# Inverse square roots of the layernorms and of layer 3 in a four-layer kernel: twelve VectorE steps in place of ScalarE's Sqrt and VectorE's reciprocal

## The chip, the cores and the metric

The kernel runs on one core of one Trainium2 chip. A core has five engines, each with its own queue: PE (TensorE, matmuls), DVE (VectorE), ACT (ScalarE), POOL (GpSimd) and SP (SyncE, which here only issues DMAs). The metric is the device time of one execution in microseconds. Times are medians of several runs.

## The reference, cut to what matters

Four layers follow each other. Each adds an attention part and a feed-forward part to `x`, which has 4 batches of 256 tokens with 256 features. Both parts read a layernorm of `x`.

```python
def _layernorm(x, axis=-1, eps=1e-05):
    m = jnp.mean(x, axis=axis, keepdims=True)
    v = jnp.var(x, axis=axis, keepdims=True)
    return (x - m) / jnp.sqrt(v + eps)

x = x + _L0_xattn_ref(_layernorm(x), ctx_2048, mask)     # plain attention over the context
x = x + _L0_ffn_ref(_layernorm(x), ...)                  # 32 experts, top 8
x = x + _L1_xattn_ref(_layernorm(x), ctx_2048, ...)      # adds a mean over the context, then a layernorm with gamma and beta
x = x + _L1_ffn_ref(_layernorm(x), ...)                  # 8 experts, top 2, and a shared one
x = x + _L2_xattn_ref(_layernorm(x), ctx_2048, ...)      # 16 heads of 128, keys and queries normed
x = x + _L2_ffn_ref(_layernorm(x), ...)                  # 4 experts, top 1
x = x + _L3_xattn_ref(_layernorm(x), ctx_2048, ...)
x = x + _L3_ffn_ref(_layernorm(x), ...)                  # quantized weights and activations
```

The attention of layer 3 has 32 heads of 8 features, and 1601 keys for each batch. Each head of each query and key is divided by its root mean square:

```python
def _rmsnorm(t):
    return t * jax.lax.rsqrt(jnp.mean(t * t, axis=-1, keepdims=True) + EPS)   # EPS = 1e-6
k_raw = context @ Wk.T; v_raw = context @ Wv.T; q = x @ Wq.T
q = _rmsnorm(q); k = _rmsnorm(k)
attn = softmax(q k^T / sqrt(8)); out = attn v
```

So an inverse square root is needed for every token of every layernorm (two columns for a tile of 128 partitions by 2 tokens), for each head of each key of layer 3 (13 key tiles by 32 heads, 416 columns a batch) and for each head of each query (64 columns a batch).

## The kernel before, in words

The tile framework orders each engine's instructions when the kernel is built, by priorities and modelled costs. On the chip an engine runs its own list in that order and waits where an input is not there yet. An instruction that waits holds all that stand behind it on its engine.

`rstd` (lines 79 to 82) makes every inverse square root of the kernel before: a Sqrt on ScalarE with scale and bias, then VectorE's reciprocal. ScalarE must load a table of functions (`ACT_TABLE_LOAD` in the profile) when it goes from Exp or another function to Sqrt, and again on the way back.

`layernorm` (line 84) is called 24 times. For each half of a tile VectorE runs `bn_stats` and `bn_aggr`; `rstd` follows on two columns, and then two `tensor_scalar` write the normed halves (line 95). Its callers are `normed` (line 115; layers 0 and 1, whose xn tiles PE transposes into `tp_ln`), `l1_xattn` (line 1195; two layernorms a batch called y and z), `turned` in layer 2 (line 1338) and layer 2's FFN (line 969).

While layers 0 and 1 run, `l2_early` (line 1206) makes the keys and values of layer 2 as filling work for PE: product, copies on ScalarE, squares (`sq_early`, one buffer), a reduce (`ss_early`) and `rstd` on 13 columns. These calls of `rstd`, those of layer 2's own keys (line 1437) and of layer 0 (line 317) are the same in both kernels.

Layer 3 works on one batch after the other (`l3`, line 1729). For each batch it goes over 8 pairs (h, u), and for each over 7 pairs of key tiles: `scores` (matmuls into `s`, then Exp on ScalarE into `e`), `values` (matmuls of the step before into `o`), and then one step of a generator, `beside` (line 1972), which prepares the next batch and finishes the batch before. Its steps are:

- `l3_kv` (line 1668), one key tile a step: four matmuls (two for each accumulation) into a PSUM bank `b`, one copy to `kr` and two to `va`. After tiles 4, 9 and 12 `l3_squares` squares a group of 5, 5 or 3 tiles (on POOL in the loop, on ScalarE in the early part) and VectorE reduces it into `ss`. After all tiles POOL multiplies `kr` by the inverse roots in four pieces, and PE transposes `kr` into `kT`.
- `queries` (line 1779): normed x, four transposes, copy to `xT`, product with wq, copy to `qr`, squares on ScalarE, reduce, inverse roots, multiply, transposes, copy to `qT`.
- `norms` (line 1772): statistics and inverse roots of x for the layernorms. It is called for batch 0 ahead of the layer, for batches 1 to 3 at the start of loop b=0, and for single batches later.
- `ffn` (line 1865) for the batch before.

In the loop all PSUM banks of these steps come from one pool with one buffer (`bank`, line 1752):

```python
ps = es.enter_context(tc.tile_pool(name="a3p", bufs=1, space=PSUM))
def bank():
    return ps.tile([P, 512], F32, name="b3", tag="tp")
```

For b > 0 the Sqrt in `queries` (line 1810) takes the keys, the queries and two columns for the old batch's layernorm at once, 482 columns; the reciprocals come in pieces of 66, 208 and 208 (lines 1811 and 1816). The keys of batch 0 have a Sqrt and a reciprocal of 416 columns of their own (line 1697).

Of the kernel before, what the change touches and what calls it, by code (L numbers as in the profile page):

```python
# [11 lines left out]
F32 = mybir.dt.float32  # L12
# [4 lines left out]
I32 = mybir.dt.int32  # L17
AF = mybir.ActivationFunctionType
ALU = mybir.AluOpType
# [4 lines left out]
P = 128  # L24
# [34 lines left out]
class Kernel:  # L59
# [19 lines left out]
    def rstd(self, out, in_, scale, eps):  # L79

        self.nc.scalar.activation(out, in_, AF.Sqrt, bias=eps, scale=scale)
        self.nc.vector.reciprocal(out, out)

    def layernorm(self, out, x):

        nc = self.nc
        st = self.small.tile([P, 2, 6], F32, name="ln_st")
        mv = self.small.tile([P, 2, 2], F32, name="ln_mv")
        rs = self.small.tile([P, 2], F32, name="ln_rs")
        for q in range(2):  # L90
            nc.vector.bn_stats(st[:, q, :], x[:, q, :])
            nc.vector.bn_aggr(mv[:, q, :], st[:, q, :])
        self.rstd(rs, mv[:, :, 1], 1.0, self.eps5)
        for q in range(2):
            nc.vector.tensor_scalar(
                out[:, q, :], x[:, q, :], mv[:, q, 0:1], rs[:, q : q + 1],
                ALU.subtract, ALU.mult,
            )
# [1569 lines left out]
    def l3_kv(self, b, st, early):  # L1668


        nc = self.nc
        ctxT = self.ctx3
        pool = self.late3 if b % 2 else self.a3
        kr = st["kr"] = self.a3.tile([P, NM, D], F32, name="kr3")
        va = st["va"] = self.va3[b % 2]
        ss = st["ss"] = self.a3.tile([P, (NM + 2) * NH3 + 2], F32, name="ss3")
        for m in range(NM):
            copy = nc.scalar.copy if early() else nc.vector.tensor_copy
            tf = self.take()
# [3 lines left out]
            copy(kr[:, m, :].rearrange("p (h d) -> p h d", d=HD3), tp[:, :, :, 0])  # L1683
            for h in range(2):
                copy(
                    va[h][:, m, : 16 * (HD3 + 1)].rearrange("p (h e) -> p h e", e=HD3 + 1)[:, :, :HD3],
                    tp[:, h * 16 : (h + 1) * 16, :, 1],
                )
            if m in (4, 9, NM - 1):
                m0 = {4: 0, 9: 5}.get(m, 10)  # L1690
                self.l3_squares(st, kr[:, m0 : m + 1, :], m0, early())
            if m == NM - 1 and b < B - 1:
                self.ctx3 = self.load_ctxT(self.a3, b + 1, 1)
            yield
        if b == 0:
            nk = NM * NH3
            self.rstd(ss[:, :nk], ss[:, :nk], 1.0 / HD3, self.eps6)
        for m0, m1 in ((0, 4), (4, 8), (8, 12), (12, NM)):
            v = kr[:, m0:m1, :].rearrange("p m (h d) -> p (m h) d", d=HD3)
            f = ss[:, m0 * NH3 : m1 * NH3, None].to_broadcast([P, (m1 - m0) * NH3, HD3])  # L1700
            nc.gpsimd.tensor_tensor(v, v, f, ALU.mult)
        yield
        yield
        yield
        kT = st["kT"] = [pool.tile([P, MP], F32, name="kT3", bufs=2) for _ in range(2)]
        for m0 in range(0, NM, 4):
            for h in range(2):
                n = min(4, NM - m0)
                copy = nc.scalar.copy if early() else nc.vector.tensor_copy
                tp = self.take().rearrange("p (m k) -> p m k", k=P)  # L1710
                for m in range(n):
                    nc.tensor.transpose(tp[:, m, :], kr[:, m0 + m, h * P : (h + 1) * P], self.ident)
                copy(kT[h][:, m0 * P : (m0 + n) * P], tp[:, :n, :].rearrange("p m k -> p (m k)"))
                yield

    def l3_squares(self, st, v, m0, early, pool=None):

        n = v.shape[1]
        sq = (pool or self.a3).tile([P, 2 if pool else 5, D], F32, name="sqq3" if pool else "sq3")
        if early:  # L1720
            self.nc.scalar.activation(sq[:, :n, :], v, AF.Square)
        else:
            self.nc.gpsimd.tensor_tensor(sq[:, :n, :], v, v, ALU.mult)
        self.nc.vector.tensor_reduce(
            st["ss"][:, m0 * NH3 : (m0 + n) * NH3], sq[:, :n, :].rearrange("p m (h d) -> p (m h) d", d=HD3),
            AX.X, ALU.add,
        )

    def l3(self, first):

# [10 lines left out]
        with ExitStack() as es:  # L1741
# [30 lines left out]
            def norms(bs):  # L1772

                for b in bs:
                    stats(b)
                v = slice(bs[0], bs[-1] + 1)
                self.rstd(rs[:, v, :], mv[:, v, :, 1], 1.0, self.eps5)

            def queries(b, st, old=None, fill=lambda n: None):

                ss = st["ss"]
                nk, nq = NM * NH3, (NM + 2) * NH3
                if old is not None:
                    stats(old)
                    nc.vector.tensor_scalar(
                        ss[:, nq:], mv[:, old, :, 1], float(HD3), HD3 * (1e-5 - 1e-6), ALU.mult, ALU.add
                    )
                elif b:  # L1790
                    nc.vector.memset(ss[:, nq:], 1.0)
                xn = normed(b, rs[:, b, :])
                fill(0)
                tp = bank().rearrange("p (k q t) -> p k q t", k=2, q=2)
# [10 lines left out]
                        self.mm(tq[:, q, :], xT[:, k, q * P : (q + 1) * P], self.wq3[:, k, :], k == 0, k == 1)  # L1805
                qr = one.tile([P, 2, D], F32, name="qr3")
                nc.vector.tensor_copy(qr, tq)
                self.l3_squares(st, qr, NM, True, one)
                part = ss if b else ss[:, nk:nq]
                nc.scalar.activation(part, part, AF.Sqrt, bias=self.eps6, scale=1.0 / HD3)  # L1810
# [161 lines left out]
            def beside(b, st):  # L1972

                if b + 1 < B:
# [40 lines left out]
            for _ in queries(0, first, None, lambda n: [next(kv) for _ in range(FIRST3[n])]):  # L2015
                pass
            busy = True
            self.take = bank
# [208 lines left out]
```

## Time and profile before

| | |
|---|---|
| median of 3 runs | 2565.55 us (2564.33 to 2566.97) |
| the profiled execution | 2571.23 us, its span 2569.2 us |
| granted PE clock over the span | 0.973 |
| busy: PE, DVE, ACT, POOL | 2429.6, 1404.4, 1310.9, 837.8 us |
| table loads on ACT | 79 of 1283 ns each, 34 of them at line 81 |
| Sqrt of a layernorm (128x2), reciprocal of it | 297 ns and 161 ns |
| Sqrt of a query (128x482) | 697 ns |
| reciprocals of 66, 208 and 416 columns | 567, 1418 and 2747 ns |

The page of the profile gives shares and counts for one execution. The timeline gives each instruction's start and duration in microseconds from the span's start, and in square brackets the idle time of its engine before it with what ended that. A group row gives the shape, the count, the busy time in us and the mean of one in ns, and then the idle time before such instructions. The layers lie at about 0 to 370 us (layer 0), 370 to 625 (its last addition and layer 1), 640 to 1925 (layer 2) and 1925 to 2569 (layer 3).

### The profile page before, as it was taken

To read this page: it belongs to the slowest core of one execution; us is meant where nothing else is said; L and a number is where in the kernel's file an instruction comes from. 1 tells how busy PE (TensorE), PEld (TensorE's weight loads), DVE (VectorE), ACT (ScalarE), POOL (GpSimd) and SP (SyncE) were. 2 spreads that over 40 slices of the span, in tenths; PEclk is the share of its full clock that TensorE was granted. 3 is DMA by queue.
4 is the path that set the end of the run, shared out by engine and by line. 5 is a ranking of instruction groups with operands and counts; after the bars stand their busy time and mean duration, and the time that the engine had idled before them with its cause. 6 is when DMAs were issued, how large, how long until landed. Compare 5 with 4: busy or idle time off the path is not lost.

```text
span 2569.2 us, 47086 instructions
## 1 busy us (share of the span) xinstructions
PE 2429.6 (95%) x17607; PEld 1507.7 (59%) x17623; DVE 1404.4 (55%) x2915; ACT 1310.9 (51%) x3000; POOL 837.8 (33%) x1516
## 2 busy tenths in 40 slices
PE   8989987899989999999999999998999999999997
PEld 5777865777645555555555555565554544544553
DVE  5453534843567777777777777763324324334323
ACT  3234434533654545454545454423336766757875
POOL 1015644213345555555555555541011001011000
PEclk9999998989999999999999999998999999999998
DMA  7165574624601111111111111004310100000000
GB/s 252 49 211 163 169 151 146 216 91 138 225 18 48 48 48 48 47 47 48 47 48 48 47 48 48 9 1 176 125 56 28 35 1 28 6 1 2 6 6 5
DMA packets 96474, 188.45 MB, mean 73 GB/s; under 512 B 15401, under 2 KB 64297, under 8 KB 95050
## 3 DMA queue, kind: packets, MB, share of 16 engines
q1 hardware_dynamic: 80102, 146.50, 16.7%
q0 software_dynamic: 10416, 28.46, 4.6%
q10 hardware_dynamic: 5732, 10.49, 1.3%
q8 instruction: 143, 2.34, 0.4%
q14 instruction: 81, 0.66, 0.1%
HBM read 137.29 MB, written 48.11 MB: 72 GB/s over the span
## 4 chain that ended last, share of the span: by engine, by line
PE 84%; DVE 5%; ACT 3%; DMA 3%; issue 2%; POOL 1%; another core or an unknown queue 1%; SPq 0%; ACTq 0%; PEld 0%; POOLq 0%; DVEq 0%; PEldq 0%
PE s L77 25%; PE o L77 24%; PE fill L1241 3%; PE f2gu L77 3%; PE b L77 3%; PE f1gu L77 2%; PE acc L77 2%; PE tpq L77 2%; PE f0gu L77 2%; PE filly L1241 2%; PE tpkv L77 2%; PE av L77 2%; PE f0y L77 2%; PE f2y L77 1%; PE f1y L77 1%
## 5 line engine op out<-in xcount | busy, mean ns | idle before, releaser
L1487 ACT ACTIVATE p<-s,nmsm 128x448 f32<-128x448 f32 (+1 forms) x512 | 326.1, 643 | 381.4 <-PE s L77 247.5
L1943 ACT ACTIVATE e<-s 128x1024 f32<-128x1024 f32 (+1 forms) x448 | 404.2, 960 | 159.6 <-PE s L77 154.5
L77 PE MATMUL o<-pT,va 128*128 128x256 f32 (+2 forms) x1920 | 434.2, 379 | 9.4 <-DVE pT L1528 7.9
L77 PE MATMUL s<-kT,qT 128*32 128x448 f32 (+1 forms) x4096 | 427.3, 558 | 11.6 <-ACT kT L1459 8.2
L77 PEld LDWEIGHTS o<-pT,va 128*128 128x128 f32 (+1 forms) x1920 | 347.5, 192 | 130.4 <-issue 89.6
L1522 POOL TENSOR_SCALAR p<-p,rm 128x448 f32<-128x448 f32 (+1 forms) x512 | 323.1, 651 | 6.2
L1483 DVE TENSOR_REDUCE nmsm<-s 128x2 f32<-128x896 f32 (+1 forms) x256 | 287.5, 1123 | 7.9
L77 PE MATMUL s<-qb,kT 32*128 32x256 f32 (+1 forms) x3328 | 268.2, 405 | 13.2 <-ACT e L1943 11.0
L1528 DVE STREAM_TRANSPOSE pT<-p 128x896 f32<-128x896 f32 (+1 forms) x256 | 270.7, 1111 | 9.4 <-POOL p L1522 8.7
L77 PEld LDWEIGHTS s<-kT,qT 128*32 128x32 f32 x4096 | 120.2, 110 | 264.0 <-issue 239.0
L77 PE MATMUL o<-e,va 128*32 128x256 f32 (+1 forms) x3328 | 236.3, 392 | 1.2 <-DVE os L2040 1.2
L77 PEld LDWEIGHTS s<-qb,kT 32*128 32x128 f32 (+1 forms) x3328 | 163.4, 181 | 105.2 <-issue 75.5
L1515 POOL TENSOR_TENSOR rm<-em,tot 32x8 f32<-32x8 f32 x256 | 54.2, 212 | 400.8 <-DVE tot L1512 389.6
L1241 PE MATMUL fill<-wkc_early,ctxT 128*128 128x256 f32 (+1 forms) x572 | 146.2, 407 | 13.4 <-ACT kT_early L1277 12.6
L77 PEld LDWEIGHTS o<-e,va 128*32 128x32 f32 (+1 forms) x3328 | 90.6, 110 | 115.1 <-issue 75.0
L1970 POOL TENSOR_TENSOR x<-x,t 128x32 f32<-128x32 f32 x64 | 14.7, 251 | 439.7 <-DVE t L1965 439.7
L1480 DVE TENSOR_TENSOR s<-s,mask 128x128 f32<-128x128 f32 (+1 forms) x256 | 84.3, 330 | 104.7 <-PE s L77 92.5
L1241 PEld LDWEIGHTS fill<-wkc_early,ctxT 128*128 128x128 f32 (+1 forms) x572 | 114.4, 203 | 35.4 <-ACT kT_early L1277 14.8
L458 POOL DMA_INDIRECT f0xr<-f0xd,f0src x95 | 90.5, 953 | 70.6 <-PE f0tph L515 18.7
L1487 ACT ACTIVATION_READ_ACCUMULATOR p<-s,nmsm 128x1 f32 x512 | 101.4, 198 | 0.0
L77 PE MATMUL f2gu<-f2wgu,f2xsT 128*128 x176 | 85.5, 611 | 0.6 <-ACT f2xsT L74 0.3
L566 POOL DMA_INDIRECT f0yt<-f0yd,f0slot x64 | 62.3, 974 | 64.1 <-DVE x L558 33.4
(488 smaller groups left out, 3500.4 us busy)
## 6 DMA issues: line engine op xcount, KB each, us to landing
ctxT<-in_ctxT SPq DMA_DIRECT2D x9, 1664.0 KB
vd<-va_early SPq DMA_DIRECT2D x96, 128.0 KB
kd<-kT_early SPq DMA_DIRECT2D x48, 256.0 KB
kT<-kd SPq DMA_DIRECT2D x16, 768.0 KB
va<-vd SPq DMA_DIRECT2D x16, 768.0 KB
f0yd<-f0ys SPq DMA_DIRECT2D x95, 128.0 KB
wq<-in_l_wq SPq DMA_DIRECT2D x16, 512.0 KB
wo<-in_l_wo SPq DMA_DIRECT2D x16, 512.0 KB
```

Source lines behind the costliest of these rows:

```text
L77: self.nc.tensor.matmul(out, lhsT, rhs, start=start, stop=stop, **kw)
L458: nc.gpsimd.indirect_dma_start(out=t, out_offset=None, in_=xd[:, :], in_offset=bass.IndirectOffsetOnAxis(ap=src[:, n : n + 1], axis=0),)
L566: nc.gpsimd.indirect_dma_start(out=yt, out_offset=None, in_=yd[:, :], in_offset=bass.IndirectOffsetOnAxis(ap=slot[:, t, r : r + 1], axis=0),)
L1241: ins = nc.tensor.matmul(tp[:rows, t, :], ctxT[u // NKV2][:, k, c0 : c0 + rows], w[u % NKV2][:, k, :], start=k == 0, stop=k == 1,)
L1480: nc.vector.tensor_tensor(sv, sv, mask[:, 2 * c : 2 * c + 2, : nt - CT, :].rearrange("p n t i -> p n (t i)"), ALU.add)
L1483: nc.vector.tensor_reduce(ms[:, 0, 2 * c : 2 * c + 2], s[:, :, : nt * 32], AX.X, ALU.max, negate=True)
L1487: nc.scalar.activation(p[:, n, : nt * 32], s[:, n, : nt * 32], AF.Exp, bias=ms[:, 0, e : e + 1], accum_out=ms[:, 1, e : e + 1],)
L1515: nc.gpsimd.tensor_tensor(r[32 * a : 32 * a + 32], e[:, a], tot, ALU.mult)
L1522: nc.gpsimd.tensor_scalar(p[:, n, : nt * 32], p[:, n, : nt * 32], r[:, e : e + 1], 1.0, ALU.mult, ALU.mult)
L1528: self.pin(nc.vector.transpose(pT[:, 2 * c : 2 * c + 2, :nt, :].rearrange("p n t i -> p n (t i)"), p[:, :, : nt * 32]))
L1943: nc.scalar.activation(e[:kr, :, :n, :], s[t][:kr, :, :n, :], AF.Exp, scale=1.0 / math.sqrt(HD3))
L1970: nc.gpsimd.tensor_tensor(xt, xt, t[:, q], ALU.add)
```

## The change

A new function `root` makes the inverse square root on VectorE alone: the argument v, a first guess from the bits of v (a shift and a subtraction from a constant as integers), and three Newton steps of three instructions. That is twelve instructions, each of which reads what the one before it wrote or the one before that.

```python
    def root(self, out, in_, scale, eps, space=None):
        vec = self.nc.vector
        n = in_.shape[1]
        if space is not None:
            space = space.rearrange("p m d -> p (m d)")
            v, y, t = (space[:, k * n : (k + 1) * n] for k in range(3))
        else:
            v, y, t = (self.small.tile([P, n], F32, name=f"root_{a}{n}", bufs=2) for a in "vyt")
        vec.tensor_scalar(v, in_, scale, eps, ALU.mult, ALU.add)
        yi = y.bitcast(I32)
        vec.tensor_scalar(yi, v.bitcast(I32), 1, None, ALU.arith_shift_right)
        vec.tensor_scalar(yi, yi, -1.0, float(0x5F3759DF), ALU.mult, ALU.add)
        for k in range(3):
            vec.scalar_tensor_tensor(t, y, -0.5, y, ALU.mult, ALU.mult)
            vec.tensor_tensor(t, t, v, ALU.mult)
            vec.scalar_tensor_tensor(out if k == 2 else y, t, 1.5, y, ALU.add, ALU.mult)
```

It takes the place of `rstd` in `layernorm`, in `norms` (one call a batch, width 2), for the keys of layer 3 and for the queries:

```diff
@@ layernorm
-        self.rstd(rs, mv[:, :, 1], 1.0, self.eps5)
+        self.root(rs, mv[:, :, 1], 1.0, 1e-5)
@@ l3_kv
-        ss = st["ss"] = self.a3.tile([P, (NM + 2) * NH3 + 2], F32, name="ss3")
+        ss = st["ss"] = self.a3.tile([P, (NM + 2) * NH3], F32, name="ss3")
...
             if m in (4, 9, NM - 1):
                 m0 = {4: 0, 9: 5}.get(m, 10)
-                self.l3_squares(st, kr[:, m0 : m + 1, :], m0, early())
+                sq = self.l3_squares(st, kr[:, m0 : m + 1, :], m0, early())
+                part = ss[:, m0 * NH3 : (m + 1) * NH3]
+                self.root(part, part, 1.0 / HD3, 1e-6, sq)
+                v = kr[:, m0 : m + 1, :].rearrange("p m (h d) -> p (m h) d", d=HD3)
+                nc.gpsimd.tensor_tensor(
+                    v, v, part[:, :, None].to_broadcast([P, (m + 1 - m0) * NH3, HD3]), ALU.mult
+                )
...
-        if b == 0:
-            nk = NM * NH3
-            self.rstd(ss[:, :nk], ss[:, :nk], 1.0 / HD3, self.eps6)
-        for m0, m1 in ((0, 4), (4, 8), (8, 12), (12, NM)):
-            v = kr[:, m0:m1, :].rearrange("p m (h d) -> p (m h) d", d=HD3)
-            f = ss[:, m0 * NH3 : m1 * NH3, None].to_broadcast([P, (m1 - m0) * NH3, HD3])
-            nc.gpsimd.tensor_tensor(v, v, f, ALU.mult)
@@ norms
-                v = slice(bs[0], bs[-1] + 1)
-                self.rstd(rs[:, v, :], mv[:, v, :, 1], 1.0, self.eps5)
+                for b in bs:
+                    self.root(rs[:, b, :], mv[:, b, :, 1], 1.0, 1e-5)
@@ queries
-            def queries(b, st, old=None, fill=lambda n: None):
+            def queries(b, st, fill=lambda n: None):
-                if old is not None:
-                    stats(old)
-                    nc.vector.tensor_scalar(
-                        ss[:, nq:], mv[:, old, :, 1], float(HD3), HD3 * (1e-5 - 1e-6), ALU.mult, ALU.add
-                    )
-                elif b:
-                    nc.vector.memset(ss[:, nq:], 1.0)
...
-                self.l3_squares(st, qr, NM, True, one)
-                part = ss if b else ss[:, nk:nq]
-                nc.scalar.activation(part, part, AF.Sqrt, bias=self.eps6, scale=1.0 / HD3)
-                nc.vector.reciprocal(ss[:, nk : nq + 2 if b else nq], ss[:, nk : nq + 2 if b else nq])
+                sq = self.l3_squares(st, qr, NM, True, one)
+                self.root(ss[:, nk:nq], ss[:, nk:nq], 1.0 / HD3, 1e-6, sq)
...
-                if b:
-                    for c in range(0, nk, nk // 2):
-                        nc.vector.reciprocal(ss[:, c : c + nk // 2], ss[:, c : c + nk // 2])
@@ beside
-                    qs = queries(b + 1, st, b - 1 if b else None)
-                    for _ in range(2):
-                        next(qs)
+                    next(kv)
+                    yield
+                    for _ in queries(b + 1, st):
                         yield
                     for _ in kv:
                         yield
-                    for _ in qs:
-                        yield
-                    nq = (NM + 2) * NH3
-                    old = [normed(b - 1, st["ss"][:, nq:])] if b else []
+                    if b:
+                        norms([b - 1])
+                    old = [normed(b - 1, rs[:, b - 1, :])] if b else []
```

The keys of layer 3 are thus normed in three groups (160, 160 and 96 columns) as soon as each group is squared and reduced, with the workspace of a root in the tile of the squares. POOL multiplies the keys in three pieces of 1280, 1280 and 768 columns. In `beside` the whole of `queries` runs one step later and before what is left of `l3_kv`, and the layernorm of the old batch is computed at its own place. In the changed program VectorE has 534 instructions more (3436 against 2902), ScalarE 65 fewer, 32 of them table loads; PE and SP have as many as before.

More of the change, by code (lines that the diff above doesn't have):

```diff
@@ L82, in rstd @@
         self.nc.vector.reciprocal(out, out)
+    def root(self, out, in_, scale, eps, space=None):
[4 more added lines that the diff above has]
+            v, y, t = (space[:, k * n : (k + 1) * n] for k in range(3))
+        else:
+            v, y, t = (self.small.tile([P, n], F32, name=f"root_{a}{n}", bufs=2) for a in "vyt")
[7 more added lines that the diff above has]
+            vec.scalar_tensor_tensor(out if k == 2 else y, t, 1.5, y, ALU.add, ALU.mult)
     def layernorm(self, out, x):
@@ L1727, in l3_squares @@
         )
+        return sq
     def l3(self, first):
@@ L2014, in l3 @@
             norms([0])
-            for _ in queries(0, first, None, lambda n: [next(kv) for _ in range(FIRST3[n])]):
+            for _ in queries(0, first, lambda n: [next(kv) for _ in range(FIRST3[n])]):
                 pass
```

## The prediction

> **What bounds the kernel now.** I read the page's busy times first, then its chain of waits, then the idle gaps of PE in the timeline, since a change that touches no matmul can only act through those gaps.
>
> ```profile
> PE 2429.6 (95%) x17607; PEld 1507.7 (59%) x17623; DVE 1404.4 (55%) x2915; ACT 1310.9 (51%) x3000; POOL 837.8 (33%) x1516
> PE 84%; DVE 5%; ACT 3%; DMA 3%; issue 2%; POOL 1%; another core or an unknown queue 1%; SPq 0%; ACTq 0%; PEld 0%; POOLq 0%; DVEq 0%; PEldq 0%
> ```
>
> PE is the bound. It works in a fixed order, and its idle gaps sum to 134.6 us. Two kinds matter here: gaps that ScalarE's square roots make, and places where PE has next to no slack over VectorE, so that more VectorE work makes a gap. Both are in layer 3, and one more is at the end of layer 1. PE's timeline at four such places:
>
> ```profile
> 515.26 1.58 PE L127 MATMUL tp_ln<-ident,xn 128*128 128x128 f32 x8 [2.01 <-DVE xn L95]
> ...
> 1947.32 1.96 PE L77 MATMUL b<-wkv,ctxT 128*128 128x512 f32 x4 [1.89 <-DVE va L1685]
> ...
> 2108.97 1.96 PE L77 MATMUL b<-wkv,ctxT 128*128 128x512 f32 x4 [0.37 <-DVE va L1685]
> ...
> 2152.08 2.08 PE L77 MATMUL s<-qb,kT 32*128 32x256 f32 x8 [3.43 <-ACT e L1943]
> ```
>
> The last of these is what the change takes away. ScalarE's timeline ahead of it:
>
> ```profile
> 2146.27 0.63 ACT L1721 ACTIVATE sqq<-qr 128x512 f32<-128x512 f32 x1 [1.66 <-DVE qr L1807]
> 2147.70 1.28 ACT L1810 ACT_TABLE_LOAD   x1 [0.80 <-DVE ss L1724]
> 2148.99 0.70 ACT L1810 ACTIVATE ss<-ss,eps 128x482 f32<-128x482 f32 x1
> 2149.71 1.28 ACT L1943 ACT_TABLE_LOAD   x1
> ```
>
> The exponentials that PE needs stand behind a wait of 0.80, a load, a Sqrt and a second load. The 2108.97 row is what the change can hurt. VectorE's timeline beside it:
>
> ```profile
> 2106.34 1.49 DVE L1724 TENSOR_REDUCE ss<-sq 128x160 f32<-128x1280 f32 x1 [2.04 <-POOL sq L1723]
> 2107.74 0.35 DVE L1923 TENSOR_SCALAR qb<-qT,mk 128x256 f32<-128x256 f32 x1
> 2108.01 0.42 DVE L1683 COPY kr<-b 128x256 f32<-128x256 f32 x1
> 2108.34 0.48 DVE L1685 COPY va<-b 128x128 f32<-128x128 f32 x2
> ```
>
> The key product lies in the only `b` bank. PE can't start the next product, nor any score or value matmul behind it, until kr and both va are copied out. The reduce of one key group already delays that by 0.37.
>
> **The price of a root.** No row of before is a root. Its twelve steps are three tensor_scalar, six scalar_tensor_tensor and three tensor_tensor. The nearest rows, by group (mean ns is the number after the comma):
>
> ```profile
> L1787 DVE TENSOR_SCALAR ss<-mv 128x2 f32<-128x2 f32 x2 | 0.3, 170 | 0.1
> L1870 DVE TENSOR_SCALAR xn<-xn 128x256 f32<-128x256 f32 x8 | 2.5, 316 | 0.0
> L275 DVE SCALAR_TENSOR_TENSOR r<-mx,r 128x1 f32<-128x1 f32 x8 | 1.3, 160 | 0.3
> L625 DVE SCALAR_TENSOR_TENSOR f0place<-f0hi,f0sf 128x64 f32<-128x64 f32 x1 | 0.2, 213 | 0.0
> L1266 DVE TENSOR_TENSOR kr_early<-kr_early,ss_early 128x128 f32<-128x128 f32 x9 | 2.6, 288 | 0.0
> L1150 DVE SCALAR_TENSOR_TENSOR x<-f2yt,f2gate,x 128x256 f32<-128x256 f32 x8 | 3.5, 480 | 4.4 <-DMA f2yt<-f2yd,f2slot 4.2
> ```
>
> Between these rows I take 0.25 and 0.32 at width 160, 0.22 and 0.25 at 96, 0.20 and 0.21 at 64, 0.17 and 0.155 at 2. Whether the next step may overlap depends on its input:
>
> ```profile
> 418.35 0.42 DVE L91 BATCH_NORM_STATS2 ln_st<-x 128x6 f32<-128x256 f32 x1
> 418.80 0.18 DVE L92 BATCH_NORM_AGGREGATE ln_mv<-ln_st 128x2 f32<-128x6 f32 x1
> ...
> 1944.75 0.40 DVE L1761 BATCH_NORM_STATS2 st<-x 128x6 f32<-128x256 f32 x1
> 1945.06 0.17 DVE L1762 BATCH_NORM_AGGREGATE mv<-st 128x2 f32<-128x6 f32 x1
> 1945.14 0.40 DVE L1761 BATCH_NORM_STATS2 st<-x 128x6 f32<-128x256 f32 x1
> ```
>
> A dependent step starts 0.03 after the end of the one before it; an independent one starts about 0.09 before it. So a lone root costs 3x0.25 + 9x0.32 + 12x0.03 = 4.0 us at width 160, 3.3 at 96, 2.9 at 64 and 2.3 at 2; interleaved small steps come at about 0.09 each. Here a rule weighs against the change. The Trainium skill, "VectorE: DVE Perf Modes", sections "The DRAIN you can't avoid" and "Rules for kernel authors", says that the next VectorE instruction doesn't issue until the pipe is empty, and to minimize the number of chained instructions. For dependent steps the trace agrees (0.03 after). For independent neighbours it does not (0.09 before). By the rule the three interleaved roots of `norms(1..3)`, 36 small steps, would take about 36x0.16 = 5.8 us; by the trace 3.2. I take the trace.
>
> **Taken away.**
> (1) Three queries: PE gaps of 2.65, 3.43 and 3.43 at 1959, 2149 and 2313, 9.5 in all. The squares (0.63 each) stay on ScalarE, so I take -9.0 (between -7.5 and -9.5). On the price of a table switch the Trainium skill, "ScalarE: Activation LUTs", section "What ACT_TABLE_LOAD costs", has 1283 ns and then a drain of some 1380, 2.66 us in all. The load here is 1.28 as it says, but the Sqrt starts 0.01 after it and no drain is seen. By the rule two switches a query would make gaps of about 6 and a gain of 18, and nearly half of the loss below would be paid for; the trace's gaps cap it at 9.5.
> (2) ScalarE waits at 1924 (va behind a Sqrt that waits for VectorE, 2.07) and at 2417 (load, Sqrt, load, 1.50): 3.6. The first gives back about 1, since the root there (2.3 in place of 0.56) leads to xn, which PE needs soon after. -2.5 (-3.6 to 0).
> (3) The other loads of the 32 removed (41 us of ScalarE at 1283 ns) end no PE gap in the trace. In layer 2's body PE has no gap over 0.7 between 743 and 1714, and ScalarE and VectorE have slack there. Counted as 0. Layer 2's FFN starts on layernorms done before; their gap (2.73 at 1735) waits for xn from x, not for its root. 0. If that cover were missing, each lone root would cost 1.7.
>
> **Added.**
> (4) Key groups of layer 3, two batches normed within loops b=1 and 2. In the changed order five root steps of group one (1.6 us), eleven of group two (3.7) and eleven of group three (3.0) stand between their reduce and what PE waits for. Group one: no slack at 2108.97, so 1.6 plus some 0.5 of steps between kr and va. Group two (beside 2130.85 in before): va is copied out at 2130.5, slack 0.35, so 3.7 + 0.3 - 0.35 = 3.6. Group three stands before the `close` of a head, slack about 1: 2.0. That is 7.7 a batch; steps that overlap their neighbours take off some 0.7. 2 x 7.0 = +14 (8 to 18).
> (5) Loop b=0, 1940 to 1957. VectorE is full there: six x additions, six bn_stats, then kr and va. Now two roots of 160 and three of width 2 come in between. From 1940: first root 3.2 (partly overlapped) ahead of kr; then a reduce of 1.5, ten steps of the second root 2.8 and some 22 small ones 2.0 ahead of the second va. Less the reduce that stood before kr in the old order, va comes 8 to 9 us later than at 1947.2, and the matmul at 1947.32 waits on it. +8 (4 to 11), with the third group ahead of the xT copy in it.
> (6) End of layer 1. The y root of the last batch shares VectorE's order with two ss_early reduces that wait for ScalarE squares of key tiles still being made. By hand the first xn moves from 514.8 to 521 to 524. PE's fills run out at 513.25 as before, so its gap of 2.01 grows by 6 to 9. +7.5 (3 to 12).
> (7) Lone roots of `norms([b-1])` ahead of kr copies in loops 1 and 2: 2.3 each against slack of one step of about 1: +2 (0 to 4). Query roots: 2.9 in place of load, Sqrt and reciprocal; in loop 0 that delays qT by about 1, later the transposes come three steps later and hide it: +1 (0 to 2).
> (8) Tail: nothing else runs. Aggregate to xn takes 0.56 now (2543.46 to 2544.02) and 2.3 then; the Tanh table load lies beside it both times. +1.8.
> (9) POOL norms the same keys in three pieces, earlier; they were never what PE waited for. SP's DMAs are the same in number; early in layer 2 a few (kd, va, wq, wo) trade places in its queue, and ScalarE's f1xd stores move with their xn, where PE waits for none of them (between 743 and 1714 it waits for nothing long). Layer 0 and the way into layer 2: +0.3 (-1 to 3).
>
> Sum: -9.0 - 2.5 + 14 + 8 + 7.5 + 2 + 1 + 1.8 + 0.3 = +23 us. It is made against the profiled run, 2571.23 us with a span of 2569.2, which stands 5.7 above the median of 2565.55. Against the median it gives 2588.
>
> **Rivals.**
> A, the likeliest (0.70): the sum above, 2588, with its own range 2576 to 2602.
> B, faster (0.12): root steps hide. One mechanism: the copies of kr and va come out ahead of the steps in time, because steps on one small tile follow each other much faster than their durations add up. It decides at about 0.09 per step in (4) and (5), the spacing of independent neighbours. Then eleven steps are 1.0, and (4) is 2x1.2, (5) 2 and (6) 0. The sum is -9.0 - 2.5 + 2.4 + 2 + 1.8 = -5, and with slack absorbing (4) -8: 2557 to 2560. For it speaks VectorE's 55% busy; against it, that each Newton step reads the one before it, and that a step of width 160 has to stream 160 elements.
> C, even (0.08): ScalarE's gaps are removed in full, and the losses of (4) to (6) come at their low ends: about 2566 to 2571.
> D, worse (0.10): VectorE's tensor_scalar slows while POOL works. The row of xn by ss (L1767), beside POOL's pieces of 2042 ns, takes 1374 ns against 486 for the same shape by rs. POOL now norms keys among the groups, so some steps and copies fall beside it; three more us in each of six groups give 2606.
> That the change doesn't do what it says is out: 65 fewer ScalarE instructions (32 of them loads) and 534 more on VectorE are in the program.
>
> **How the numbers follow.** The likeliest case gives 2588. About 0.2%, 5.1 us, is what a measurement of this kernel can tell from no change. Faster by more than that (below 2560.4): nearly all of B, 0.11. Within it: the rest of B and most of C, 0.08. Slower (above 2570.7): A, D and the top of C, 0.81. The range runs from 2566 (C's low end) to 2607 (D's value); outside lie B and half of D, under 0.2.
>
> **What would show it.** In the trace after: no table load ahead of e in layer 3, and the three gaps at L1943 gone or under 1; new gaps of 1.5 to 4 on the `b` matmul, released by va, three a batch; the one near 1947 grown to 8 or more; the tp_ln gap near 513 grown to 8 or more; the tail longer by 1.8. The forecast is wrong if root steps of width 160 take under 0.2 each, if the `b` gaps stay under 0.5, or if the first xn of layer 1's FFN isn't later.

## The result, and the profile after

The changed kernel takes 2593.08 us (median of 5 runs, 2591.83 to 2594.07), the kernel before 2565.55 us in the same session (2564.33 to 2568.84). The ratio is 1.0105 (95% interval 1.009 to 1.012): slower by 27.5 us. The profiled execution of the changed kernel has a span of 2592.2 us, 23.0 more than before's. The forecast was 2588.

The page of the changed kernel, first the busy times and then the chain of waits:

```profile
PE 2433.3 (94%) x17623; PEld 1506.3 (58%) x17623; DVE 1491.4 (58%) x3449; ACT 1261.6 (49%) x2935; POOL 843.7 (33%) x1512
...
PE 82%; DVE 8%; DMA 3%; issue 3%; ACT 2%; POOL 2%; another core or an unknown queue 1%; SPq 0%; ACTq 0%; DVEq 0%; POOLq 0%
```

ScalarE lost 49 us of work and VectorE got 87. In the chain the share of PE fell by 2 points, that of ScalarE by 1, and VectorE's rose from 5% to 8%: PE waits for VectorE where it didn't. PE's timeline at the places that the prediction showed, and at two new ones:

```profile
518.61 1.23 PE L146 MATMUL tp_ln<-ident,xn 128*128 128x128 f32 x4 [10.68 <-DVE xn L114]
...
1957.07 3.78 PE L77 MATMUL b<-wkv,ctxT 128*128 128x512 f32 x4 [3.60 <-DVE va L1704]
...
2105.79 3.23 PE L77 MATMUL b<-wkv,ctxT 128*128 128x512 f32 x4 [2.20 <-DVE va L1704]
...
2124.78 1.96 PE L77 MATMUL b<-wkv,ctxT 128*128 128x512 f32 x4 [2.26 <-DVE va L1704]
...
2150.36 3.42 PE L77 MATMUL b<-wkv,ctxT 128*128 128x512 f32 x4 [3.62 <-DVE va L1704]
...
2174.85 0.66 PE L1829 MATMUL b<-ident,qr 128*128 128x128 f32 x4 [1.59 <-DVE qr L1821]
```

In order: the first xn of layer 1's FFN (2.01 before, 10.68 now), the second key product of loop 0 (1.89 before), the old batch's layernorm (no gap before), key groups one (0.37 before) and two (none before), and the query. The last four come again in loop 2, 170 us later. The query's place on ScalarE is as it was meant to be, with no load between square and exponentials:

```profile
2169.69 0.63 ACT L1739 ACTIVATE sqq<-qr 128x512 f32<-128x512 f32 x1 [1.65 <-DVE qr L1817]
2170.23 2.88 ACT L1948 ACTIVATE e<-s 128x1024 f32<-128x1024 f32 x4
```

VectorE's timeline for key group two of loop 1, ahead of the gap of 3.62, shows the cause (the first and the last of the root's steps, with the copies):

```profile
2144.05 1.49 DVE L1742 TENSOR_REDUCE ss<-sq 128x160 f32<-128x1280 f32 x1 [2.04 <-POOL sq L1741]
2145.57 0.24 DVE L94 TENSOR_SCALAR sq<-ss 128x160 f32<-128x160 f32 x1
...
2149.17 0.42 DVE L1702 COPY kr<-b 128x256 f32<-128x256 f32 x1
2149.50 0.32 DVE L101 SCALAR_TENSOR_TENSOR ss<-sq 128x160 f32<-128x160 f32 x1
2149.73 0.48 DVE L1704 COPY va<-b 128x128 f32<-128x128 f32 x2
```

Eleven steps stand between the reduce and the copy of kr, from 2145.57 to 2149.25: 3.7 us, the number that the prediction worked out.

To see where the 23 us of span went, take the start of the same matmul in both traces and subtract: PE's lag over before. Its growth by stage, in us, for this and the experiments' kernels (stages by the times of before's trace; a minus is time gained). The experiments ran on other chips, where all kernels take some 40 us less (before too, by its medians), nearly all of it between 370 and 505 us; so only growth from 506 us on is set beside each other. Two executions of the changed kernel (the first row and e11) differ by up to 2 us in a stage.

| kernel | ratio to before | 506-620 | layer 2's FFN, 1716-1905 | loop 0, to 2068 | loop 1, to 2200 | loop 2, to 2365 | loop 3, to 2532 |
|---|---|---|---|---|---|---|---|
| changed | 1.0105 | +9.5 | -4.5 | +10.4 | +6.7 | +6.6 | -2.1 |
| e1 layernorms back | 1.0092 | -2.7 | -3.1 | +10.7 | +6.4 | +6.7 | -2.3 |
| e2 layernorms alone | 1.0036 | +11.5 | -3.1 | -1.7 | 0.0 | 0.0 | 0.0 |
| e3 one step for keys | 1.0094 | +11.5 | -4.4 | +6.8 | +2.8 | +4.2 | -2.1 |
| e4 key roots on POOL | 1.0084 | +9.2 | -3.9 | +12.6 | -1.0 | -0.9 | -2.4 |
| e5 multiplication late | 1.0114 | +11.6 | -4.4 | +7.7 | +6.6 | +6.6 | -2.1 |
| e6 own workspace | 1.0129 | +9.3 | -4.5 | +10.5 | +6.4 | +6.6 | -2.4 |
| e7 one key root, late | 0.9999 | +0.1 | -1.6 | -1.3 | +0.7 | -1.3 | +0.3 |
| e8 POOL, from before | 1.0014 | 0.0 | -2.3 | +3.9 | -2.4 | -1.3 | +1.9 |
| e9 two steps, own workspace | 0.995 | 0.0 | -3.0 | +0.1 | -5.1 | -5.3 | -2.4 |
| e10 no multiplication | 1.0116 | +11.5 | -4.3 | +4.2 | +6.6 | +6.7 | -2.3 |
| e11 changed again | 1.0119 | +11.5 | -4.5 | +12.1 | +5.0 | +6.6 | -2.1 |
| e12 e9 with three steps | 1.0001 | +0.1 | -1.9 | +5.0 | -0.8 | -1.1 | -2.4 |

In the changed kernel the rest is -6.2 before 506 us, +0.6 from 620 to 1716 (nothing in layer 2's body) and +2.0 in the tail; with these the row adds up to the 23 us. The stage from 620 to 1716 is left out of the table: it runs from -3.0 to +3.3, also in e7 and e8, which change nothing there.

A stage can grow in two ways: PE waits longer, or PE runs the same matmuls at a lower granted clock, which in these traces is at every moment either full or half. The windows view tells the two apart, and this matters for loop 0 below.

### The profile page after: what moved, and what is told of

The parts are those of the page before. It is cut to its first block, busy times and chain, and to the rows that moved or that the text cites. A ratio compares the mean times of both kernels' runs of the same rounds, so it can differ in the third digit from the quotient of the medians.

```text
span 2592.2 us, 47539 instructions
## 1 busy us (share of the span) xinstructions
PE 2433.3 (94%) x17623; PEld 1506.3 (58%) x17623; DVE 1491.4 (58%) x3449; ACT 1261.6 (49%) x2935; POOL 843.7 (33%) x1512
## 3 DMA queue, kind: packets, MB, share of 16 engines
q1 hardware_dynamic: 80102, 146.50, 16.5%
## 4 chain that ended last, share of the span: by engine, by line
PE 82%; DVE 8%; DMA 3%; issue 3%; ACT 2%; POOL 2%; another core or an unknown queue 1%; SPq 0%; ACTq 0%; DVEq 0%; POOLq 0%
PE s L77 24%; PE o L77 23%; PE fill L1260 3%; PE f2gu L77 3%; PE b L77 3%; PE tpq L77 2%; PE f1gu L77 2%; PE acc L77 2%; PE f0gu L77 2%; PE filly L1260 2%; PE tpkv L77 2%; PE av L77 2%; PE f2y L77 1%; PE f0y L77 1%; DMA f0xr<-f0xd,f0src 1%
```

## Experiments: the two halves of the change

**e1** puts `layernorm` of the changed kernel back; **e2** changes only `layernorm` of the kernel before.

```diff
 e1 (from the changed kernel)
-        self.root(rs, mv[:, :, 1], 1.0, 1e-5)
+        self.rstd(rs, mv[:, :, 1], 1.0, self.eps5)
 e2 (from before, with root() added)
-        self.rstd(rs, mv[:, :, 1], 1.0, self.eps5)
+        self.root(rs, mv[:, :, 1], 1.0, 1e-5)
```

> The changed kernel with layernorm() back on Sqrt and reciprocal; layer 3 as changed. Theory T (roots delay PE at the end of layer 1; the lag of -6 us that the changed kernel's trace has before 505 us is chance of DMA-paced stages): the tp_ln gap near 508 goes from 10.7 to about 2, and the time from 2593 to about 2583. Rival R (the layernorms' missing table loads gave the -6 us before 505 and the -4.5 us in layer 2's FFN, and pay for the gap): about 2593, within 2.

> The kernel before with only layernorm() on the root of twelve steps; layer 3 untouched. Theory T: about 2575 (2565.5 + 10), the tp_ln gap of 10 to 11 us is there, layer 3 is as before. Rival R: about 2566.

Measured: e1 1.0092 of before (1.0072 to 1.0113), e2 1.0036 (1.0023 to 1.0048). PE's row at the first xn of layer 1's FFN, e1 and then e2:

```profile
471.97 1.52 PE L146 MATMUL tp_ln<-ident,xn 128*128 128x128 f32 x8 [2.01 <-DVE xn L114]
```

```profile
480.50 1.23 PE L146 MATMUL tp_ln<-ident,xn 128*128 128x128 f32 x4 [10.68 <-DVE xn L114]
```

The gap goes and comes with the layernorms' roots: in e2 it is the 10.68 of the changed kernel, in e1 the 2.01 of before. Layer 3 costs its 21 us in e1 with the layernorms back. So theory T holds by the gaps, and in e2 by the time as well. The time of e1 alone doesn't decide: theory T had 2583 against 2565.5, a ratio of 1.0068, and the rival 2593, a ratio of 1.0107; the interval holds the rival's value and not theory T's. About a third of the loss is the layernorms at the end of layer 1, two thirds are layer 3, and the two ratios together (1.0128) meet that of the whole (1.0105 and 1.0119). The lag of -6.2 us before 506 us is no gain of the change: in the experiments, kernels with and without layernorm roots both stand between -41 and -45 there. Nor does the gain of 4.5 in layer 2's FFN come mostly from shorter waits: PE waits 0.9 less there, and it runs the same 643 matmuls in 175.5 us in place of 179.1, with less time at half clock. A gain of 1.6 and 2.3 is also seen in e7 and e8, where nothing is changed there. What of the rest belongs to which root stays open.

**e3** gives the key groups one Newton step in place of three.

```diff
-                self.root(part, part, 1.0 / HD3, 1e-6, sq)
+                self.root(part, part, 1.0 / HD3, 1e-6, sq, 1)   # steps=1
```

> The changed kernel with one Newton step in place of three for layer 3's key groups (keys less exactly normed), so each key root has 6 steps, not 12. Theory T (the root's own time on VectorE ahead of the key copies makes the b gaps): 1.9 us less in each group that stands ahead of a copy; the gap of group two 3.6 to about 1.7, group one about as it was (its five steps ahead of kr remain), loop 0 about 3 less; 2593 to about 2586. Rival (the new order of queries and of POOL's pieces makes the gaps): unchanged, 2592 to 2594.

Measured: 1.0094 (1.007 to 1.0119). PE at group two of loop 1:

```profile
2108.94 1.95 PE L77 MATMUL b<-wkv,ctxT 128*128 128x512 f32 x4 [1.59 <-DVE va L1704]
```

3.62 became 1.59 for six steps less (6 x 0.33 = 2.0). Group one stays at 2.03, as its five steps ahead of kr remain. Layer 3's three loops grow by 13.7 in place of 23.7. The ratio alone doesn't tell e3 from the changed kernel; the gap does. For group two the root's own time ahead of the copy makes the gap; that the new order of queries and multiplications doesn't, and that the same holds for group one, is left to e4, which keeps that order.

**e4** moves the key groups' roots to POOL, but for the two integer steps.

```diff
-                self.root(part, part, 1.0 / HD3, 1e-6, sq)
+                self.root_pool(part, part, 1.0 / HD3, 1e-6, sq)
+    def root_pool(...):   # v, and for each Newton step three tensor_tensor and one tensor_scalar, on POOL
+        vec.tensor_scalar(yi, v.bitcast(I32), 1, None, ALU.arith_shift_right)
+        vec.tensor_scalar(yi, yi, -1.0, float(0x5F3759DF), ALU.mult, ALU.add)
```

> The changed kernel with the key groups' roots on GpSimd but for the two integer steps, which stay on VectorE (13 instructions on POOL a group). Theory T: the b gaps of groups one and two (2.26 and 3.6) fall under 0.7, loop 0 loses about 6, so about 2577. Rival (POOL's work at the same time slows VectorE's copies, or VectorE's integer steps wait for POOL ahead of the copies): over 2588, with gaps ahead of the b matmuls released by va.

Measured: 1.0084 (1.0063 to 1.0105). In loops 1 and 2 the theory nearly holds: groups one and two fall to 1.10 (forecast under 0.7) and 0.64, and each loop is 1 us faster than before. The order of queries and multiplications is that of the changed kernel, so it was the roots' place on VectorE that made these gaps. PE waits 1 to 2 us longer in each loop than in before, but it never stands at half clock there. In loop 0 the theory fails. ScalarE's row there:

```profile
1913.85 1.27 ACT L1755 ACTIVATE sq<-kr 128x1280 f32<-128x1280 f32 x1 [9.67 <-POOL ss L117]
```

The square of the next group waits 9.67 for POOL's root, since the root works in the tile of the squares and there is one such tile. The exponentials stand behind it, and PE waits 5.21 for them.

## Experiments: loop 0

In the changed kernel loop 0 grew by 10.4, twice what the prediction had. Two suspects, each read from a timeline. First, one of VectorE's steps that took longest there, and POOL's instruction in the same stretch:

```profile
1948.80 2.17 DVE L94 TENSOR_SCALAR root_v<-mv 128x2 f32<-128x2 f32 x1
```

```profile
1948.54 2.41 POOL L1714 TENSOR_TENSOR kr<-kr,ss 128x1280 f32<-128x1280 f32 x1 [26.13 <-DVE st L1780]
```

Its neighbours of two columns take 0.15. This one starts after POOL's instruction and ends with it (1950.97 and 1950.95). Two more steps of the loop do the same: one takes 2.36 beside the next multiplication, one 1.37 beside POOL's squares. **e5** moved POOL's multiplication behind all groups. **e10** leaves it out, so that its keys aren't divided by their root mean square. **e6** gave the roots a tile of their own, the second suspect, since ScalarE's square of a group waited 2.57 for VectorE's root.

```diff
 e5: the four POOL pieces of the kernel before, after the loop over m, in place of the three in it
 e10: the three POOL pieces are gone
-                nc.gpsimd.tensor_tensor(
-                    v, v, part[:, :, None].to_broadcast([P, (m + 1 - m0) * NH3, HD3]), ALU.mult
-                )
 e6:
-                self.root(part, part, 1.0 / HD3, 1e-6, sq)
+                self.root(part, part, 1.0 / HD3, 1e-6, self.a3.tile([P, 3, 160], F32, name="root3"))
```

> The changed kernel with the roots per group as they are, but POOL's multiplication of the keys in four pieces after all groups, where before had it. In the changed kernel's trace three short VectorE steps in loop 0 took 2.17, 2.36 and 1.37 us, each up to the end of a POOL multiplication, where such a step takes 0.15; one qb step in each of loops 1 and 2 took 2.39. Theory T (VectorE steps between SBUF tiles are held while POOL multiplies, and this made loop 0 lose more than its roots' own time): those steps fall to their usual time and layer 3 gets shorter by 3 to 6 us, so 21 to 24 us over before in place of 27. Rival (only the roots' own time counts): 26 to 28 over before.

> The changed kernel with a tile of its own as workspace for the key groups' roots, in place of the tile of the squares. Theory T (in loop 0 ScalarE's squares of the next group wait for the root that works in their tile, and the exponentials behind them make the gap of 2.91 us near 1947): that gap goes, 2 to 3 us less, so about 24 over before. Rival (the exponentials wait for something else): the gap stays and the time is that of the changed kernel, 26 to 28 over before.

> The changed kernel without POOL's multiplication of the keys (left out: layer 3's keys aren't divided by their root mean square; the roots are still computed). In e5 the late pieces still ran beside VectorE's short steps of loop 0, three of which took 1.44, 1.93 and 1.38 us. Theory T (a VectorE step between SBUF tiles is held until POOL's instruction ends): with no multiplication there, no width-2 step takes over 0.5 us but the one beside POOL's squares (1.4), and PE's lag over before from 1904 us to 2528 us, 21.6 us in the changed kernel, falls to 16 to 18. Rival (the long steps are something else, or they cost PE nothing): the lag stays at 20 to 22.

Measured: e5 1.0114 (1.0097 to 1.0131), e6 1.0129 (1.0112 to 1.0146), e10 1.0116 (1.0096 to 1.0136); these intervals don't tell the three from the changed kernel in the same session as e10 (e11, 1.0119), so the stages decide.

e5 didn't test what it was meant to: the late pieces start when their roots are there, and three short steps still took 1.44, 1.93 and 1.38. In e10 none of the root's steps of loop 0 is long but one beside POOL's squares (1.45). PE's row there:

```profile
1915.53 2.93 PE L77 MATMUL b<-wkv,ctxT 128*128 128x512 f32 x3 [2.28 <-DVE va L1704]
```

From the reduce of group one to this matmul VectorE has no idle time over 0.3. The stretch takes 17.8 us in the changed kernel (1939.27 to 1957.07), 17.8 in e11 and 15.8 in e10 (1899.77 to 1915.53). So the step held by POOL costs 2.0 us (2.17 less 0.15) at the wait that ends last; the second one (2.36) comes behind the copies. The Trainium skill, "SBUF — State Buffer", section "Who interferes with whom", says the same in words: VectorE and GpSimd share a pair of ports, and the second one blocks fully until the first is done; the end of the held step agrees to 0.02 us. Loops 1 and 2 don't change (6.6, 6.7), where such a step came too (a qb of 2.39) but nothing was waiting on it.

Yet loop 0 grows by 4.2 in e10 in place of 10.4 and 12.1, which is 6 to 8 less and not 2. The windows view over the whole of loop 0 shows the rest, for the changed kernel, e11 and e10 (stretch, length, busy time of PE, PEld, DVE, ACT and POOL with instructions, then the PE clock granted as a share of full speed, DMA share and GB/s):

```profile
1904.35:2077.77 173.42, 157.05 (x1643) 83.86 (x1641) 78.61 (x220) 105.23 (x146) 18.32 (x24) 0.94 0.12 39
1870.50:2045.55 175.05, 158.54 (x1643) 84.03 (x1641) 78.51 (x220) 105.14 (x146) 18.36 (x24) 0.93 0.12 38
1866.54:2033.75 167.21, 151.78 (x1643) 81.68 (x1641) 74.41 (x220) 105.28 (x146) 11.93 (x21) 0.98 0.12 40
```

The matmuls are the same 1643. PE is idle for 16.4, 16.5 and 15.4 us: 1 us less in e10. The other 5 to 7 us are busy time, at a granted clock of 0.98 in place of 0.94 and 0.93; the kernel before has 153.31 busy and 0.97 there. A slower PE also arrives later at a wait, so that a part of VectorE's 2.0 us shows as busy time. Whether POOL's hold is also why PE stands at half clock for longer isn't shown: in e5, with three steps held, the clock is 0.96 and the loop grows by 7.7.

e6's second suspect is real and didn't pay. The 2.91 gap behind ScalarE's square is gone, and the key product that follows waits for VectorE all the longer:

```profile
1919.30 2.93 PE L77 MATMUL b<-wkv,ctxT 128*128 128x512 f32 x3 [9.14 <-DVE va L1704]
```

9.14 in place of 2.91 and 3.60. The last wait of the stage was VectorE's, as the prediction had it; the ScalarE wait lay inside it. PE waits 3 us more over the loop (19.4 in place of 16.4), and the loop grows by 10.5 as in the changed kernel only because the same matmuls took 154.1 in place of 157.1.

**e11** is the changed kernel again, as the base of e9 and e10.

> The changed kernel once more, on the chip of the other kernels of this call, as the base for them. Theory T: 1.008 to 1.013 of before, with the tp_ln gap of 10.7, the three b gaps of 2.2, 2.3 and 3.6 in each of loops 1 and 2, and 21 to 22 us of lag in layer 3. Rival (these gaps belong to the one profiled execution): gaps at other places or under half of these sizes.

Measured: 1.0119 (1.0097 to 1.0141), gaps of 10.68, 2.19, 2.27 and 3.62 at the same places, 21.5 us of lag in layer 3. Theory T holds.

## Experiments: can the loads be saved for less?

**e7** starts from before and has two roots a batch on VectorE: 66 columns for the query with the old layernorm, and 416 for the keys, behind the last key product.

```diff
-                nc.scalar.activation(part, part, AF.Sqrt, bias=self.eps6, scale=1.0 / HD3)
-                nc.vector.reciprocal(ss[:, nk : nq + 2 if b else nq], ss[:, nk : nq + 2 if b else nq])
+                self.root(ss[:, nk : nq + 2 if b else nq], ..., 1.0 / HD3, 1e-6, sq)
 in l3_kv, after the loop over m:
+            self.root(ss[:, :nk], ss[:, :nk], 1.0 / HD3, 1e-6, self.a3.tile([P, 5, D], F32, name="sq3"))
```

> The kernel before with layernorms as before, and two roots on VectorE in layer 3: 66 columns for a query with the old batch's layernorm, and 416 columns for the keys of batches 1 to 3, behind the last key product instead of in groups. Theory T (the loss comes from where the roots stand, ahead of copies that PE waits for, and not from their sum on VectorE; the 416 root is 7 us of VectorE): the three e gaps of 2.65, 3.43 and 3.43 go, no new b gap over 1, so 5 to 9 us faster than before. Rival (VectorE time itself is what is lost, or the key transposes now wait for root and POOL): 0 to 8 us slower than before.

Measured: 0.9999 (0.9989 to 1.0009). The three ScalarE gaps are 1.1 or gone, and yet nothing is won. VectorE and PE in loop 1:

```profile
2096.38 0.38 DVE L94 TENSOR_SCALAR sq<-ss 128x416 f32<-128x416 f32 x1
...
2100.00 0.22 DVE L2000 TENSOR_TENSOR t<-b,r 128x64 f32<-128x64 f32 x1
```

```profile
2100.37 0.63 PE L1836 MATMUL b<-ident,xn 128*128 128x128 f32 x4 [2.56 <-DVE t L2000]
```

The root isn't late: its place in VectorE's order is right behind the last reduce, and now the product of `close` (`t`) stands behind seven of its steps. Then `os` is late by 1.83. The 3.43 that ScalarE gave are taken by these two. My theory, that place alone matters, was wrong in this form; the rival's reason, key transposes that wait, isn't seen either.

**e8** starts from before, with the query root on VectorE and key groups on POOL (as in e4, batch 0 too). **e9** adds a workspace of its own, two Newton steps in place of three (a less exact root), and roots on VectorE for layer 2's FFN and for batch 2 in the last loop. **e12** is e9 with three steps.

```diff
 e9 (from e8; the edits of the two layernorms are left out here)
-                self.root_pool(part, part, 1.0 / HD3, 1e-6, sq)
+                self.root_pool(part, part, 1.0 / HD3, 1e-6, self.a3.tile([P, 3, 160], F32, name="root3"))
-        for k in range(3):      # root and root_pool
+        for k in range(2):
 e12 (from e9)
-        for k in range(2):
+        for k in range(3):
```

> The kernel before with layernorms as before, the query root of 66 columns on VectorE, and key roots by groups on POOL with its multiplication (workspace in the squares' tile, batch 0 too). Theory T (with no key root on VectorE and the old layernorm folded into the query root, the gaps of 2.2, 2.26 and 3.6 and the e gaps all go in loops 1 and 2: 3.4 us less than before in each; loop 0 loses 3 to 6 by ScalarE's squares that wait for POOL's root in their tile): 0 to 5 us faster than before. Rival (POOL's longer work holds VectorE's steps everywhere): over 5 us slower.

> From the kernel before: key roots by groups on POOL with a workspace of their own (two integer steps on VectorE), the query root of 66 columns on VectorE, layernorm roots on VectorE only in layer 2's FFN and for batch 2 in the last loop; two Newton steps in place of three everywhere; all other layernorms on ScalarE as before. Theory T (roots pay where PE doesn't wait for VectorE; in the kernel of e8 the gap of 6.8 us in loop 0 was ScalarE waiting for the squares' tile): that gap under 3, loops 1 to 3 together 5 to 7 less than before, layer 2's FFN 1 to 3 less; 4 to 9 us faster than before. Rival (POOL's roots hold VectorE's copies and what is gained is lost there): within 2 of before.

> The kernel of e9 with three Newton steps everywhere, as in the changed kernel. Theory T (e9's gain comes from where the roots stand, not from the step left out): faster than before by 5 to 10 us, ratio 0.996 to 0.998; loop 0 loses 1 to 3 us more than in e9, since POOL's root of a group is 2 us longer and VectorE's integer steps of the next group wait for it. Rival (the step left out made the gain): within 3 us of before.

Measured: e8 1.0014 (1.0005 to 1.0023), e9 0.995 (0.9934 to 0.9966), e12 1.0001 (0.9993 to 1.0009). e8 missed its forecast (0 to 5 us faster): it is slower, as loop 0 cost 3.9, loops 1 and 2 gave 2.4 and 1.3 where 3.4 each was forecast, and loop 3 cost 1.9. e9 missed one part of its own: the gap of loop 0 was to fall under 3 us. e9 beats both kernels in its session, before by 10.5 us and the changed kernel (e11) by 44.5. I had put the gain to place and workspace; e12 shows that it is the step left out. By the ratios, each to before on its own chip, the step is worth 13 us. In the traces loops 0 to 2 and layer 2's FFN are 14 us shorter in e9: PE waits 8 us less, and the rest is the same work at a higher clock. Loop 1 tells how the waits go, first in VectorE and PE of e12:

```profile
2102.22 0.95 DVE L1761 TENSOR_REDUCE ss<-sq 128x96 f32<-128x768 f32 x1 [3.19 <-POOL sq L1760]
```

```profile
2104.55 0.63 PE L1835 MATMUL b<-ident,xn 128*128 128x128 f32 x4 [1.85 <-DVE t L1999]
```

and then in VectorE and PE of e9:

```profile
2092.48 0.95 DVE L1761 TENSOR_REDUCE ss<-sq 128x96 f32<-128x768 f32 x1 [1.18 <-POOL sq L1760]
```

```profile
2094.90 0.66 PE L1835 MATMUL b<-ident,xn 128*128 128x128 f32 x4
```

In e12 POOL is still at work for group two when group three's squares are due (they start at 2100.72, 2.1 us after their keys are copied). The reduce waits 3.19 in VectorE's order with `close` behind it, and PE waits 1.85. With four POOL instructions less the squares find POOL free, and PE has no gap. e9's loop 0 stays level with before for a like reason: an integer step on VectorE waits 3.72 for POOL, whose next root stands behind a multiplication of 2.41, and PE waits 6.91. No run removes that wait.

## Why the prediction was right, point by point

- **The price of a root** held: 3.7 us of eleven steps at 160 columns (forecast 3.7), 0.24 and 0.32 a step; a lone root of two columns 2.37 from 1924.46 to the start of xn at 1926.83 (forecast 2.3).
- **(1), (2) the ScalarE gaps.** The three behind a Sqrt are gone as said; loop 3 gives back 2.1 (forecast 1.5). But loop 0 got a new ScalarE gap of 2.91, as a square waits 2.57 for the root that works in its tile, and around 1924 another gap came (2.24, PE for xn), so the 1 us there wasn't won.
- **(4) the key groups.** Groups one and two: 2.26 and 3.62 (forecast 2.1 and 3.6). Group three makes no gap in place of 2.0, probably since the transposes of xn stand a step later and its `close` isn't needed as early; no run tests that. In its place came the query's 1.59, which (7) had as hidden by the same move.
- **(5) loop 0** was sized at +8 for VectorE and about +5 net with the gains of the loop. The matmul of 1947.32 came 10.4 later relative to the loop's start, and the loop ended at 10.4 net. Two terms were missing. One is POOL, 2.0 us at that matmul: rival D, at the wrong place. It named the row (1374 against 486 ns) but spread its price over the groups; it fell on the small steps of loop 0. The other is the clock, which the prediction had at nothing: PE's busy time for the same 1643 matmuls rose from 153.3 to 157.1.
- **(6) the end of layer 1**: +7.5, measured +9.5 (e11: +11.5), with the first xn at 518.2, 10.3 us after PE's fills ran out at 507.9. The size was near, the mechanism only half as told. The two `ss_early` reduces do stand inside the root of y (2.9 us in place of 2.3), but VectorE waits for nothing there. From the end of y's statistics to the first xn it needs 14.5 us in place of 7.8: for the steps of the roots of y and z, and for three operations on y that take 2.10 and 1.41 in place of 0.73 and 0.69, beside POOL's multiplications from 506.58 to 510.52. And PE's fills ran out 2.0 sooner after y's statistics than in before.
- **(7)** the lone layernorm root of loops 1 and 2: 2.20 each (forecast +2 for both; mis-sized by half). **(8)** the tail: +1.8, as forecast. **(3)** layer 2's body: 0, as forecast; layer 2's FFN gained 4.5 where the step had 0, 3.6 of it in PE's busy time.
- **The sum** came out at +23 against 23.0 of span by luck, as misses cancel: loops 0 to 2 cost about 9 more than the terms, the end of layer 1 2 more, and stages before 506 and in layer 2's FFN gave 11 that were in no term. The medians, which don't rest on one execution, differ by 27.5. What was right is the mechanism (roots ahead of the copies and of xn that PE waits for) and, within 2 us, the gaps of each key group.
- **The rivals.** B is out: dependent steps came 0.28 to 0.36 apart at 160 columns, not 0.09. The rule of one step after another was right for these, and the trace's 0.07 to 0.09 for independent neighbours was right too: between 1953 and 1956 two roots of width 2 and one of 160 run interleaved. The section that the prediction set against this (the Trainium skill, "VectorE: DVE Perf Modes", "The DRAIN you can't avoid") itself adds that a next operation that is not held starts earlier, so page and trace need not disagree. C is out by the interval, which begins at 1.009. D's size (three more us in each of six groups) isn't seen: the loops 1 and 2 of e10, without POOL's multiplication, grow as in the changed kernel.

## What to carry to other kernels

Count the instructions that come between a copy that frees a bank and the copy before it: an operation taken off an idle-looking engine and given to another at 55% costs nothing on average and its full length at each such place. Before moving work to VectorE, look at which of PE's waits already end there with little or no slack; before moving it to POOL, look at what VectorE does between two SBUF tiles in that stretch. Before a stage's growth is put down to a cause, split it into PE's idle time and the busy time of the same matmuls. And where a version wins, take apart the edits that it joins, as e12 did with e9: the gain may belong to the one that was thought a detail.

## What the runs showed of the hardware that was not expected

A gap of PE can cost more than its length. The granted clock after before's query gap of 3.43 and after the changed kernel's gap of 3.62, each as one row of the windows view:

```profile
2152.00:2158.00 6.00, 5.92 (x44) 2.62 (x48) 6.00 (x9) 3.71 (x6) 6.00 (x4) 0.50 0.01 3
```

```profile
2150.00:2154.00 4.00, 3.64 (x8) 1.26 (x12) 2.70 (x4) 0.00 (x0) 2.37 (x1) 0.59 0.00 0
```

Six microseconds at half clock after 3.43 of waiting are 3 us more, so such a gap costs nearly twice what the prediction took for it. The gap of 2.20 was followed by 0.78 from 2103 to 2109 (four matmuls of 128x512 in 3.23 where they take 1.96), and that of 2.26 by full clock. In loops 1 and 2 of these two traces gains and losses of this kind cancel: in the clock's record before stands at half clock once for 6.83 us in each loop, the changed kernel twice for 3.41. In loop 0 they don't cancel (0.97 and 0.94).

Length alone doesn't decide. The same gap of loop 1, 2.19 long, was followed by full clock in e11 (1.00 from 2071 to 2077). And in all the traces the stretches at half clock last 3.41 us or a whole multiple of it, but for those that the end of the trace cuts off. The Trainium skill, "TensorE: Matmul & The Clock Gate", section "What's actually happening", has the clock halved after an idle window of about 3.4 us that runs free of the kernel. The lengths, and the same gap with and without a price, fit a window that runs free; but gaps of 2.20, and of 1.85 in e12 (0.66 from 2104 to 2109), were enough here, and they are shorter than the window.
